# Layer 3 of a four-layer network on one Trainium2 core: mean square from moments, norm steps and output copies on ScalarE, last rows collected third quarter first

## The chip, the cores and the metric

The kernel runs on one core of one Trainium2 chip. Its engines are named as the profile names them: PE is TensorE, with PEld for its weight loads, DVE is VectorE, ACT is ScalarE, POOL is GpSimd and SP is SyncE, which here issues most of the transfers. The metric is the device time of one execution in microseconds (us), the median over several runs; lower is better.

## The reference

The input `x` has shape (4, 1024, 128) in float32. Four layers follow, each an attention-like mixer and a feed-forward part, each added to its input and followed by a layer norm without parameters. Layers 1, 2 and 3 end in a mixture of experts; the change lies in layer 3 and in the end of layer 2.

```python
def _layernorm(x, axis=-1, eps=1e-05):
    m = jnp.mean(x, axis=axis, keepdims=True)
    v = jnp.var(x, axis=axis, keepdims=True)
    return (x - m) / jnp.sqrt(v + eps)
...
# layer 2, experts: top 2 of 8, a shared matrix plus low-rank parts, 512 wide
# layer 3, mixer: query = the normed x
    rms = jnp.linalg.norm(query, axis=-1, keepdims=True) * e ** (-0.5)
    x = query / (rms + EPS)
    u = jax.nn.silu(jnp.einsum('nbe,fe->nbf', x, u_w) + u_b)
    v = jax.nn.silu(jnp.einsum('nbe,fe->nbf', x, v_w) + v_b)
...
    y = _toeplitz_mix(vh, pos, zero, neg)        # along the batch axis of 4, by head
...
    return jnp.einsum('nbf,ef->nbe', u * y, o_w) + o_b + query
# layer 3, experts: top 4 of 32, 128 wide, and a shared expert 512 wide
    logits = flat @ router_w.T + router_bias
    scores = jax.nn.softmax(logits, axis=-1)
    topk_scores, topk_idx = jax.lax.top_k(scores, TOPK)
    topk_scores = topk_scores / jnp.clip(topk_scores.sum(-1, keepdims=True), 1e-12, None)
    h = jax.nn.silu(flat @ gate_w[e]) * (flat @ up_w[e])       # for each chosen expert e
    out = sum_e topk_scores[e] * (h @ down_w[e])
    out = out + jax.nn.silu(flat @ sgate_w.T) * (flat @ sup_w.T) @ sdown_w.T
...
x = _layernorm(x + L3_attn(x)); x = _layernorm(x + L3_ffn(x))
```

The mixer of layer 3 thus works on rows that a layer norm has just left, and wants each row's root of the mean square.

## The kernel before, in words

`self.x` holds the 4096 rows in SBUF as 32 tiles of 128 rows by 128 columns; `self.xT` holds the transposed copy. The sequence is cut into four quarters of 256 positions; a quarter of all four batch rows is 8 tiles (`QT`). A tile's number is `quarter * 8 + batch_row * 2 + half`.

**Parts.** Layer 3 works in three parts: `a` is quarters 0 and 1 (16 tiles), `b` is quarter 2, `c` is quarter 3 (8 tiles each). Layer 2's experts work in parts `a2` (quarters 0 and 1), `m2` (quarters 2 and 3 of batch rows 0 and 1) and `n2` (quarters 2 and 3 of batch rows 2 and 3). Within `n2` the order is row 2: quarter 2 (indices 0, 1), quarter 3 (2, 3); row 3: quarter 2 (4, 5), quarter 3 (6, 7).

**How a mixture of experts runs.** A routing step (`l3_route`) makes logits, softmax, a top-4 mask by rounds of maximum and match-replace, and then `positions`: for each row and each of its experts, a place in a list in DRAM that is sorted by expert (`posl3a`, `posl3b`, `posl3c`; for layer 2 `posl2m` and `posl2n`), and the weights `wk`. `spread` then writes the rows of x to that list (`l3ra`, `l3rb`, `l3rc`), one indirect DMA of 128 rows at a time, 4 for a tile, issued by POOL in `indirect` (L1297). `small_experts` loads the list in groups of 4 tiles (`xg`, by SP), turns them (PE, then an ACT copy to `xgT`), multiplies by gate and up weights into `gu`, applies the activation on ACT (`sg`, L1729) and the product on DVE (`hg`, L1730), turns that (`hT`, a DVE copy, L169), multiplies by the down weights into `yp`, copies this PSUM result to `yg` and has SP store it to `l3ya`, `l3yb` or `l3yc`. Part a has 20 such groups, b and c have 12 each. The copy to `yg` is on ACT in odd groups (L1744) and on DVE in even groups (L1747). `collect` gathers a tile's results again (`yt`, again POOL, L1297, 4 indirect DMAs a tile for layer 3 and 2 for layer 2) and adds them to x, weighted, on DVE (L1388). The buffers `yt` come from a pool of 8 or 5; when they are full, the next gather waits for the adds of the oldest. Before the first group of experts there is a shared expert (`l3_shared`).

After the likely number of groups the kernel tests on the device whether the lists are longer (`rest_of`, a branch on `usedl3a` and its like). Instructions after that branch in the program can't begin before it.

**Norms.** `norm` (L185) takes a list of tiles, computes mean and variance of each with DVE's batch-norm instructions into `mv`, then `rstd`: with `by="act"` as a square root on ACT and a reciprocal on DVE (L195, L196), with `by="dve"` by three Newton steps on DVE (`rsqrt`, L171). The last step, `(x - mean) * rstd`, is one DVE instruction for each tile (L205). `finish` and `close` make the final norm and store the output.

**Layer 3's mixer** is `l3_attn` (L1548), a generator that does a quarter at a time: first norm, then for each half quarter (4 tiles) the squares and their sum on DVE (L1584, L1585), the root (Newton on DVE for part a, `exps=True`; ACT for parts b and c), the scaled rows, their transposes, the projections u and v, the mix along the batch axis on DVE (L1628), the output projection, the second norm and the transposes for the router.

**Order.** Every step is a Python generator that emits instructions and yields a planned cost in us. `mix(main, side)` advances the side generators when the main one has yielded enough cost, so the yields decide where side work lands in each engine's in-order queue. `abreast` interleaves generators by their yields, `chain` concatenates, and `press` runs side work alone until a name is listed. The part of `all` around the change, shortened:

```python
on = served(chain(rows_in(a2), onward(a, True)), (..., routed(m2)), (..., routed(n2)))
run(mix(l2_attn(1), on))
run(mix(l2_experts(m2, wall), on))
on = chain(on, rows_in(m2))
run(mix(l2_experts(n2, wall), on))
press(on, listed("l3a"))
on = chain(on, rows_in(n2), l3_attn(b), l3_route(b),
    abreast(chain(spread(b), when("made l3a"), last(a, yp)), chain(l3_attn(c), l3_route(c))),
    spread(c), when("made l3b"), last(b, yp))
run(mix(chain(l3_shared(a), l3_experts(a)), on, 0.75)); press(on, listed("l3b"))
run(mix(chain(l3_shared(b), l3_experts(b)), on, 0.75)); press(on, listed("l3c"))
run(mix(chain(l3_shared(c), l3_experts(c)), on)); run(close(c, yp))
```

`onward(a)` is part a's mixer, routing and spread. `rows_in` collects layer 2's results of a part, through a pool `l2y...` of its own with 8 buffers on the right side of SBUF; `last(a)` collects layer 3's results of part a and finishes its rows, through the pool `l3y` of 8 buffers. The yields keep POOL's order as written: spread of a, rows of m2, rows of n2, spread of b, results of a, spread of c, results of b, results of c.

Of the kernel before, what the change touches and what calls it, by code (L numbers as in the profile page):

```python
# [14 lines left out]
AF = mybir.ActivationFunctionType  # L15
ALU = mybir.AluOpType
AX = mybir.AxisListType
# [3 lines left out]
P = 128  # L21
B, L, D = 4, 1024, 128
# [8 lines left out]
QT = NT // NQT  # L31
# [10 lines left out]
E2, F2, R2, K2 = 8, 512, 16, 2  # L42
# [32 lines left out]
class Kernel:  # L75
# [106 lines left out]
            ts(t, t, -0.5, 1.5, ALU.mult, ALU.add)  # L182
            tt(y, y, t, ALU.mult)

    def norm(self, tiles, by="act"):  # L185

        nc, n = self.nc, len(tiles)
        mv = self.tile(self.small, [P, n, 2], f"mv{n}")
        for t, x in enumerate(tiles):
            st = self.tile(self.small, [P, 6], "bn")  # L190
            nc.vector.bn_stats(st, x)  # L191
            nc.vector.bn_aggr(mv[:, t, :], st)  # L192
        rstd = self.tile(self.small, [P, n], f"rstd{n}")
        if by == "act":
            nc.scalar.activation(rstd, mv[:, :, 1], AF.Sqrt, bias=self.eps)  # L195
            nc.vector.reciprocal(rstd, rstd)  # L196
        else:
            ve = self.tile(self.small, [P, n], f"ve{n}")
            nc.vector.tensor_scalar(ve, mv[:, :, 1], LN_EPS, None, ALU.add)
            if by == "pool":  # L200
                nc.gpsimd.tensor_tensor(rstd, ve, self.mhalf[:, :n], ALU.pow)
            else:
                self.rsqrt(rstd, ve)
        for t, x in enumerate(tiles):
            nc.vector.tensor_scalar(x, x, mv[:, t, 0:1], rstd[:, t : t + 1], ALU.subtract, ALU.mult)  # L205

    def quarter(self, q):

# [1165 lines left out]
                        in_=self.zero.unsqueeze(1).to_broadcast([P, tl - at, D]),  # L1374
                    )

    def collect(self, lay, part, k, yp, first=0, nt=None):

        nc = self.nc
        pos, wk = self.route[lay + part.name][:2]  # L1380
        assert f"made {lay}{part.name}" in self.listed
        ys = self.lists[lay, part.name][1]
        late = []

        def add():
            t, yt, _ = late.pop(0)
            for i in range(k):
                nc.vector.scalar_tensor_tensor(  # L1388
                    self.x[:, part.order[t], :], yt[:, i, :], wk[:, t, i : i + 1], self.x[:, part.order[t], :],
                    ALU.mult, ALU.add,  # L1390
                )

        for t in range(first, first + (nt or part.nt)):
            yt = self.tile(yp, [P, k, D], "yt")
            for i in range(k):
                self.indirect(
                    out=yt[:, i, :], out_offset=None, in_=ys,
                    in_offset=bass.IndirectOffsetOnAxis(ap=pos[:, t, i : i + 1], axis=0),
                )

            late.append((t, yt, self.moved_by + 4.0))
            if len(late) == yp.bufs:
                while late[0][2] > self.now:
                    yield (1.0,)
                add()
            yield (1.26 * k,)
        while late:
            while late[0][2] > self.now:
                yield (1.0,)
            add()  # L1410
            yield (0.36 * k,)
# [136 lines left out]
    def l3_attn(self, part, exps=False):  # L1548


        nc, tc, x, xT, col = self.nc, self.tc, self.x, self.xT, self.col
        stt = nc.vector.scalar_tensor_tensor
        NC = D13 // P
        with ExitStack() as ctx:
# [17 lines left out]
                stt(dst, pz, col["l3_b"][:, i : i + 1], dst, ALU.add, ALU.add)  # L1572

            for q in range(part.q0, part.q0 + part.nq):
                s = slice(q * QT, (q + 1) * QT)
                self.norm(self.quarter(q), by="dve" if exps else "act")
                yield (7.0,)
                xq = self.tile(vp, [P, QC], "xq")
                rms = self.tile(self.small, [P, QT], "rms")
                for g in range(2):  # L1580
                    sg = slice(q * QT + g * 4, q * QT + g * 4 + 4)
                    r = rms[:, g * 4 : g * 4 + 4]
                    sq = self.tile(vp, [P, 4, D], "sq")
                    nc.vector.tensor_tensor(sq, x[:, sg, :], x[:, sg, :], ALU.mult)  # L1584
                    nc.vector.tensor_reduce(r, sq, AX.X, ALU.add)  # L1585
                    if exps:

                        ri = self.tile(self.small, [P, 4], "rmsi")
                        v = self.tile(self.small, [P, 4], "rmsv")
                        nc.vector.tensor_scalar(v, r, 1e-30, None, ALU.max)  # L1590
                        self.rsqrt(ri, v)
                        nc.vector.tensor_tensor(r, r, ri, ALU.mult)
                    else:
                        nc.scalar.activation(r, r, AF.Sqrt)
                    nc.vector.tensor_scalar(r, r, float(np.float32(D ** -0.5)), 1e-8, ALU.mult, ALU.add)
                    nc.vector.reciprocal(r, r)
                    yield (4.0,)
                    nc.vector.tensor_tensor(sq, x[:, sg, :], r.unsqueeze(2).to_broadcast([P, 4, D]), ALU.mult)

                    stt(  # L1600
                        x[:, sg, :], x[:, sg, :], 2.0, self.row["l3_ob"].unsqueeze(1).to_broadcast([P, 4, D]),
                        ALU.mult, ALU.add,
                    )
                    yield (2.3,)
                    self.transposes(
                        ps, xq[:, g * BLK : (g + 1) * BLK], [sq[:, k, :] for k in range(4)], on_act=not exps, tag="s"
                    )
                    yield (2.3,)
                u = self.tile(vp, [P, NC, B, TQ], "u")
                for c in range(NC):  # L1610
                    v = self.tile(vp, [P, B, TQ], "v")
                    for i, dst in ((1, v), (0, u[:, c])):
                        for g in range(2):
                            pz = self.tile(ps, [P, BLK], "s")
                            self.mm(pz, wuv[:, i, c * P : (c + 1) * P], xq[:, g * BLK : (g + 1) * BLK])
                            silu(dst[:, 2 * g : 2 * g + 2, :].rearrange("p b t -> p (b t)"), pz, i * NC + c)
                            yield (2.3,)

                    cf = col["toep"][:, c * 7 : (c + 1) * 7]
                    for i in range(B):  # L1620
                        y = self.tile(vp, [P, TQ], "y", bufs=1 if exps else 2)
                        for j in range(B):
                            lag = i - j
                            a = lag if lag >= 0 else 3 - lag
                            if j == 0:
                                nc.vector.tensor_scalar(y, v[:, j, :], cf[:, a : a + 1], None, ALU.mult)
                            else:
                                stt(y, v[:, j, :], cf[:, a : a + 1], y, ALU.mult, ALU.add)  # L1628
                        if exps:
                            stt(u[:, c, i, :], u[:, c, i, :], 0.25, y, ALU.mult, ALU.mult)  # L1630
                        else:
                            nc.vector.tensor_tensor(u[:, c, i, :], u[:, c, i, :], y, ALU.mult)
                        yield (3.0,)
                for g in range(2):
                    py = self.tile(ps, [P, 4, D], "s")
                    for k in range(4):
                        b, h = (g * 4 + k) // 2, k % 2
                        for c in range(NC):
                            self.mm(py[:, k, :], u[:, c, b, h * P : (h + 1) * P], wo[:, c, :], c == 0, c == NC - 1)
                    sg = slice(q * QT + g * 4, q * QT + g * 4 + 4)  # L1640
                    nc.vector.tensor_tensor(x[:, sg, :], py, x[:, sg, :], ALU.add)
                    yield (3.0,)
                self.norm(self.quarter(q), by="dve" if exps else "act")
                yield (6.0,)
                for g in range(2):
                    self.turned(ps, q * QT + g * 4, on_act=not exps, tag="s")
                    yield (2.3,)
# [51 lines left out]
    def small_experts(self, lay, ne, part, wall):  # L1699

        nc = self.nc
# [3 lines left out]
        with ExitStack() as ctx:  # L1705
# [31 lines left out]
            def down(g):  # L1737
# [2 lines left out]
                for i in range(4):  # L1740
                    pm = self.mm(py[:, i, :], hT[:, i * P : (i + 1) * P], wall[:, bass.ds(es[i] * (3 * P) + 2 * P, P)])
                yg = self.tile(gp, [P, 4, D], "yg")
                if g % 2:
                    nc.scalar.copy(yg, py)  # L1744
                    marks = (pm,)
                else:
                    marks = (pm, nc.vector.tensor_copy(yg, py))  # L1747
# [120 lines left out]
    def all(self):  # L1868
# [4 lines left out]
        with ExitStack() as ctx:  # L1873
# [36 lines left out]
            with ExitStack() as c3:  # L1910
                with ExitStack() as c2:
# [6 lines left out]
                    self.run(self.mix(self.l2_experts(n2, wall), on, drain=False))  # L1918
                self.press(on, listed("l3a"))
                yp = self.pool(c3, "l3y", 8)  # L1920
                on = self.chain(
                    on, self.rows_in(n2), self.l3_attn(b), self.l3_route(b),
                    self.abreast(
                        self.chain(self.spread("l3", b, K3), self.when(listed("made l3a")), self.last(a, yp)),
                        self.chain(self.l3_attn(c), self.l3_route(c)),
# [192 lines left out]
```

## Time and profile before

| | us |
|---|---|
| median of 3 runs | 2064.29 (2057.93 to 2067.41) |
| the profiled execution's own time | 2440.36 |
| its span (first to last instruction), mean granted clock 0.813 | 2438.2 |
| PE busy in it | 1619.9 (66%) |
| DVE busy, 3732 instructions | 1303.3 (53%) |
| ACT busy, 1114 instructions | 789.9 (32%) |
| POOL busy, 701 instructions | 774.0 (32%) |

The profiled execution is 18% longer than the timed ones. Durations and places below are those of the profiled execution. Busy time is the time in which an engine executed instructions; shares are of the span. Stages in it: layer 2's attention, second half, ends about 1641; m2's experts run to about 1730, n2's to 1892; part a's shared expert to 1932 and its 20 groups of experts to 2034; part b's experts from 2106 to 2231; part c's to 2380; the last norms and stores end at 2438.

### The profile page before, as it was taken

The numbers are of one execution on the slowest core, as the hardware profiler recorded it, in microseconds if no ns is written. First come the engines' busy times: TensorE is split into PE (matmuls) and PEld (weight loads), VectorE is DVE, ScalarE is ACT, GpSimd is POOL, SyncE is SP. The second block draws the span as 40 slices with busy tenths as digits, with TensorE's granted clock in tenths as the row PEclk, the third lists the DMA queues.
The fourth block names the chain that finished last, engine by engine and source line by source line (L and its number), as shares of the span: only waits on it lengthen the run. The fifth ranks groups of instructions, "written<-read, shape, count | busy, mean of one in ns | idle before, by whom it ended". The sixth has DMA issues, their size and how long they took to land. (4 is left out here: it accounts for less than half of the span.)

```text
span 2438.2 us, 27135 instructions
## 1 busy us (share of the span) xinstructions
PE 1619.9 (66%) x9017; PEld 962.6 (39%) x9017; DVE 1303.3 (53%) x3732; ACT 789.9 (32%) x1114; POOL 774.0 (32%) x701
## 2 busy tenths in 40 slices
PE   7535776875661775687968787887853898267080
PEld 3214333753320344545623232345532586154070
DVE  8767795655570564324535665464711378247053
ACT  5511372322230432222336454642211254122030
POOL 5531285145227002224132002002164201736704
PEclk9766787988785888888979898988876998577595
DMA  9930002334101014312120000031141141223132
GB/s 308 288 104 0 13 33 82 117 120 159 60 31 52 14 73 142 100 48 70 44 96 21 1 1 17 2 117 35 42 174 40 44 127 45 71 71 96 51 100 59
DMA packets 215530, 187.10 MB, mean 77 GB/s; under 512 B 16528, under 2 KB 194064, under 8 KB 214864
## 3 DMA queue, kind: packets, MB, share of 16 engines
q1 hardware_dynamic: 194672, 142.29, 18.5%
q0 software_dynamic: 20704, 42.86, 5.7%
q8 instruction: 84, 1.38, 0.2%
q14 instruction: 70, 0.57, 0.1%
HBM read 88.49 MB, written 96.60 MB: 76 GB/s over the span
## 5 line engine op out<-in xcount | busy, mean ns | idle before, releaser
L1051 ACT ACTIVATE pr<-sc 128x1024 f32<-128x1024 f32 x288 | 279.6, 1021 | 326.1 <-PE sc L157 197.7
L157 PE MATMUL gu<-ld,xgT 128*128 x640 | 172.1, 413 | 81.9 <-issue 36.6
L157 PE MATMUL sc<-qm,kT 32*128 32x512 f32 (+3 forms) x1536 | 200.2, 564 | 15.9 <-ACT pr L1051 12.0
L157 PE MATMUL s<-pr,va 128*32 128x512 f32 (+3 forms) x1536 | 177.3, 531 | 46.0 <-issue 27.9
L157 PEld LDWEIGHTS gu<-ld,xgT 128*128 128x128 f32 x640 | 123.6, 204 | 109.5 <-issue 48.0
L157 PE MATMUL gu<-wall,xgT 128*128 x304 | 161.0, 657 | 3.2 <-ACT xgT L167 2.0
L1057 DVE TENSOR_TENSOR pr<-pr,ld 128x512 f32<-128x512 f32 (+1 forms) x160 | 92.5, 581 | 101.3 <-ACT pr L1051 98.8
L169 DVE COPY hT<-tp 128x512 f32<-128x512 f32 x118 | 81.0, 686 | 120.7 <-PE tp L165 50.4
L165 PE MATMUL tp<-ld,hg 128*128 128x128 f32 x624 | 100.6, 285 | 50.4 <-DVE hT L169 35.4
L157 PEld LDWEIGHTS sc<-qm,kT 32*128 32x128 f32 x1536 | 85.5, 200 | 119.5 <-issue 66.6
L165 PE MATMUL tp<-ld,xg 128*128 128x128 f32 x396 | 66.3, 295 | 90.9 <-issue 50.7
L165 PEld LDWEIGHTS tp<-ld,hg 128*128 128x128 f32 x624 | 80.1, 147 | 104.8 <-DVE hT L169 42.2
L167 ACT COPY xgT<-tp 128x512 f32<-128x512 f32 x99 | 58.0, 587 | 195.4 <-PE tp L165 126.9
L1730 DVE TENSOR_TENSOR hg<-sg,gu 128x256 f32<-128x256 f32 x160 | 65.7, 416 | 102.5 <-ACT sg L1729 94.8
L1494 ACT ACTIVATE sg<-gu 128x512 f32<-128x512 f32 x76 | 45.2, 597 | 226.3 <-PE gu L157 115.3
L1297 POOL DMA_INDIRECT l1ra<-x,posl1a x64 | 95.6, 1494 | 60.5 <-DVE posl1a L1272 41.3
L1729 ACT ACTIVATE sg<-gu 128x256 f32<-128x256 f32 x160 | 60.6, 384 | 157.3 <-PE gu L157 85.7
L157 PE MATMUL pu<-xT,ld 128*128 128x512 f32 x104 | 65.0, 719 | 60.1 <-issue 58.5
L1297 POOL DMA_INDIRECT yt<-l1yr,posl1r x64 | 60.7, 948 | 139.2 <-DVE x L1388 78.8
L157 PEld LDWEIGHTS s<-pr,va 128*32 128x32 f32 x1536 | 38.7, 113 | 156.6 <-issue 110.6
L1496 DVE TENSOR_TENSOR hg<-sg,gu 128x512 f32<-128x512 f32 x76 | 51.8, 681 | 87.2 <-ACT sg L1494 43.9
L1297 POOL DMA_INDIRECT l1rr<-x,posl1r x64 | 61.7, 964 | 99.6 <-DVE posl1r L1272 80.4
(443 smaller groups left out, 3551.7 us busy)
## 6 DMA issues: line engine op xcount, KB each, us to landing
wall<-wall SPq DMA_DIRECT2D x16, 768.0 KB
l3ra<-zero SPq DMA_DIRECT2D x1, 6144.0 KB
ld<-in_l_w SPq DMA_DIRECT2D x2, 3072.0 KB
wall<-we SPq DMA_DIRECT2D x24, 256.0 KB
ld<-in_l_w SPq DMA_DIRECT2D x1, 6144.0 KB
l1ra<-zero SPq DMA_DIRECT2D x1, 5120.0 KB
l1rr<-zero SPq DMA_DIRECT2D x1, 5120.0 KB
xg<-l3ra SPq DMA_DIRECT2D x20, 256.0 KB
```

Source lines behind the costliest of these rows:

```text
L157: return self.nc.tensor.matmul(out, lhsT, rhs, start=start, stop=stop)
L165: nc.tensor.transpose(pt[:, k * P : (k + 1) * P], s, self.ident)
L167: nc.scalar.copy(dst, pt[:, : n * P])
L169: nc.vector.tensor_copy(dst, pt[:, : n * P])
L1051: nc.scalar.activation(pr, sc[h], AF.Exp)
L1057: nc.vector.tensor_tensor(d, d, cst["tril"].unsqueeze(1).unsqueeze(1).to_broadcast([P, 2, n, P]), ALU.mult)
L1297: ins = self.nc.gpsimd.indirect_dma_start(**kw)
L1494: nc.scalar.activation(sg, gu[:, 0, :], AF.Silu)
L1496: nc.vector.tensor_tensor(h, sg, gu[:, 1, :], ALU.mult)
L1729: nc.scalar.activation(sg, pg[:, :, 0, :], AF.Silu)
L1730: nc.vector.tensor_tensor(h[:, 2 * c : 2 * c + 2, :], sg, pg[:, :, 1, :], ALU.mult)
```

## The change

Four things are changed. (1) In `l3_attn` the mean square comes from the norm's own moments: after `(x - mean) * rstd` a row's mean square is variance times rstd squared, so `rms = sqrt(var) * rstd`, 8 wide at once; the squares and their sums are gone, and in part a one Newton chain 8 wide stands in place of two 4 wide per quarter. In parts b and c both norms' last steps are ACT instructions with a scale and a bias, for which one DVE instruction makes `off = -mean * rstd`. The planned costs of these steps become smaller (7 to 6, two times 4 to one time 2, and 6 to 5). (2) The output copy `yg` of layer 3's experts is on ACT in every group. (3) `collect` can take a list of tiles, and the rows of n2 are collected with quarter 2 of both batch rows first (indices 0, 1, 4, 5); then part b's mixer and routing run abreast with the collection of quarter 3 (2, 3, 6, 7). (4) For this the pool `l3y` is used in place of n2's own pool.

```diff
--- before.py
+++ after.py
@@ -182,7 +182,8 @@
             ts(t, t, -0.5, 1.5, ALU.mult, ALU.add)
             tt(y, y, t, ALU.mult)
 
-    def norm(self, tiles, by="act"):
+    def norm(self, tiles, by="act", on_act=False):
+
 
         nc, n = self.nc, len(tiles)
         mv = self.tile(self.small, [P, n, 2], f"mv{n}")
@@ -201,8 +202,15 @@
                 nc.gpsimd.tensor_tensor(rstd, ve, self.mhalf[:, :n], ALU.pow)
             else:
                 self.rsqrt(rstd, ve)
+        if on_act:
+            off = self.tile(self.small, [P, n], f"off{n}")
+            nc.vector.scalar_tensor_tensor(off, mv[:, :, 0], -1.0, rstd, ALU.mult, ALU.mult)
         for t, x in enumerate(tiles):
-            nc.vector.tensor_scalar(x, x, mv[:, t, 0:1], rstd[:, t : t + 1], ALU.subtract, ALU.mult)
+            if on_act:
+                nc.scalar.activation(x, x, AF.Identity, bias=off[:, t : t + 1], scale=rstd[:, t : t + 1])
+            else:
+                nc.vector.tensor_scalar(x, x, mv[:, t, 0:1], rstd[:, t : t + 1], ALU.subtract, ALU.mult)
+        return mv, rstd
 
     def quarter(self, q):
 
@@ -1374,7 +1382,7 @@
                         in_=self.zero.unsqueeze(1).to_broadcast([P, tl - at, D]),
                     )
 
-    def collect(self, lay, part, k, yp, first=0, nt=None):
+    def collect(self, lay, part, k, yp, first=0, nt=None, which=None):
 
         nc = self.nc
         pos, wk = self.route[lay + part.name][:2]
@@ -1390,7 +1398,7 @@
                     ALU.mult, ALU.add,
                 )
 
-        for t in range(first, first + (nt or part.nt)):
+        for t in which or range(first, first + (nt or part.nt)):
             yt = self.tile(yp, [P, k, D], "yt")
             for i in range(k):
                 self.indirect(
@@ -1572,29 +1580,27 @@
                 stt(dst, pz, col["l3_b"][:, i : i + 1], dst, ALU.add, ALU.add)
 
             for q in range(part.q0, part.q0 + part.nq):
-                s = slice(q * QT, (q + 1) * QT)
-                self.norm(self.quarter(q), by="dve" if exps else "act")
-                yield (7.0,)
+                mv, rstd = self.norm(self.quarter(q), by="dve" if exps else "act", on_act=not exps)
+                yield (6.0,)
                 xq = self.tile(vp, [P, QC], "xq")
+
                 rms = self.tile(self.small, [P, QT], "rms")
+                if exps:
+
+                    v = self.tile(self.small, [P, QT], "rmsv")
+                    nc.vector.tensor_scalar(v, mv[:, :, 1], 1e-30, None, ALU.max)
+                    self.rsqrt(rms, v)
+                    nc.vector.tensor_tensor(rms, rms, mv[:, :, 1], ALU.mult)
+                else:
+                    nc.scalar.activation(rms, mv[:, :, 1], AF.Sqrt)
+                nc.vector.tensor_tensor(rms, rms, rstd, ALU.mult)
+                nc.vector.tensor_scalar(rms, rms, 1e-8, None, ALU.add)
+                nc.vector.reciprocal(rms, rms)
+                yield (2.0,)
                 for g in range(2):
                     sg = slice(q * QT + g * 4, q * QT + g * 4 + 4)
+                    sq = self.tile(vp, [P, 4, D], "sq")
                     r = rms[:, g * 4 : g * 4 + 4]
-                    sq = self.tile(vp, [P, 4, D], "sq")
-                    nc.vector.tensor_tensor(sq, x[:, sg, :], x[:, sg, :], ALU.mult)
-                    nc.vector.tensor_reduce(r, sq, AX.X, ALU.add)
-                    if exps:
-
-                        ri = self.tile(self.small, [P, 4], "rmsi")
-                        v = self.tile(self.small, [P, 4], "rmsv")
-                        nc.vector.tensor_scalar(v, r, 1e-30, None, ALU.max)
-                        self.rsqrt(ri, v)
-                        nc.vector.tensor_tensor(r, r, ri, ALU.mult)
-                    else:
-                        nc.scalar.activation(r, r, AF.Sqrt)
-                    nc.vector.tensor_scalar(r, r, float(np.float32(D ** -0.5)), 1e-8, ALU.mult, ALU.add)
-                    nc.vector.reciprocal(r, r)
-                    yield (4.0,)
                     nc.vector.tensor_tensor(sq, x[:, sg, :], r.unsqueeze(2).to_broadcast([P, 4, D]), ALU.mult)
 
                     stt(
@@ -1640,8 +1646,8 @@
                     sg = slice(q * QT + g * 4, q * QT + g * 4 + 4)
                     nc.vector.tensor_tensor(x[:, sg, :], py, x[:, sg, :], ALU.add)
                     yield (3.0,)
-                self.norm(self.quarter(q), by="dve" if exps else "act")
-                yield (6.0,)
+                self.norm(self.quarter(q), by="dve" if exps else "act", on_act=not exps)
+                yield (5.0,)
                 for g in range(2):
                     self.turned(ps, q * QT + g * 4, on_act=not exps, tag="s")
                     yield (2.3,)
@@ -1740,7 +1746,7 @@
                 for i in range(4):
                     pm = self.mm(py[:, i, :], hT[:, i * P : (i + 1) * P], wall[:, bass.ds(es[i] * (3 * P) + 2 * P, P)])
                 yg = self.tile(gp, [P, 4, D], "yg")
-                if g % 2:
+                if lay == "l3" or g % 2:
                     nc.scalar.copy(yg, py)
                     marks = (pm,)
                 else:
@@ -1918,8 +1924,13 @@
                     self.run(self.mix(self.l2_experts(n2, wall), on, drain=False))
                 self.press(on, listed("l3a"))
                 yp = self.pool(c3, "l3y", 8)
+
                 on = self.chain(
-                    on, self.rows_in(n2), self.l3_attn(b), self.l3_route(b),
+                    on, self.collect("l2", n2, K2, yp, which=(0, 1, 4, 5)),
+                    self.abreast(
+                        self.chain(self.l3_attn(b), self.l3_route(b)),
+                        self.collect("l2", n2, K2, yp, which=(2, 3, 6, 7)),
+                    ),
                     self.abreast(
                         self.chain(self.spread("l3", b, K3), self.when(listed("made l3a")), self.last(a, yp)),
                         self.chain(self.l3_attn(c), self.l3_route(c)),
```

## The prediction

> **What bounds the kernel now.** I read the page's busy shares first, then the windows of 50 us over the part that the change touches, then the waits there, then the queue of POOL.
>
> ```profile
> PE 1619.9 (66%) x9017; PEld 962.6 (39%) x9017; DVE 1303.3 (53%) x3732; ACT 789.9 (32%) x1114; POOL 774.0 (32%) x701
> ```
>
> No engine is full over the span, so the stages have to be read one by one. Nothing moves before the second half of layer 2's attention, so only the last 900 us matter. Columns of the next view: stretch, its length, busy time of PE, PEld, DVE, ACT and POOL with instruction counts, granted clock, DMA share, GB/s.
>
> ```profile
> 1900.00:1950.00 50.00, 42.95 (x204) 29.59 (x204) 16.90 (x36) 9.64 (x18) 15.25 (x16) 0.90 0.17 48
> 1950.00:2000.00 50.00, 45.86 (x292) 39.76 (x291) 34.40 (x94) 30.24 (x55) 0.00 (x0) 1.00 0.43 129
> 2000.00:2050.00 50.00, 44.23 (x252) 36.09 (x251) 40.19 (x128) 25.07 (x42) 0.00 (x0) 0.87 0.22 65
> 2050.00:2100.00 50.00, 29.51 (x116) 16.80 (x114) 24.91 (x91) 11.08 (x17) 27.67 (x28) 0.79 0.12 44
> 2100.00:2150.00 50.00, 8.97 (x20) 4.94 (x20) 13.01 (x36) 3.41 (x6) 35.87 (x37) 0.55 0.27 75
> 2250.00:2300.00 50.00, 8.94 (x43) 5.85 (x41) 1.20 (x3) 0.60 (x1) 37.81 (x41) 0.60 0.20 59
> ```
>
> Two kinds of stage alternate. From 1932 to 2037 layer 3's experts of part a run: PE is busy for 45.9 of 50 us, DVE for 34 to 40, ACT for 25 to 30. What DVE gives up there buys nothing by itself. Around 2100 and 2275 PE has 9 of 50 us and POOL 36 to 38: POOL issues gathers and scatters one after another, and everything else waits for their data. The waits and the instructions of the scatter of part b's rows (`l3rb`) say what holds POOL up:
>
> ```profile
> POOL l3rb L1297 <- DVE posl3b L1272: 119.1, 1, 119.1
> POOL yt L1297 <- DVE x L1388: 78.9, 7, 53.3
> POOL l3ra L1297 <- DVE posl3a L1272: 67.4, 1, 67.4
> ...
> L1297 POOL DMA_INDIRECT l3rb<-x,posl3b x32: 957/962/1262, 2064.1 to 2104.2; - x32
> L1328 SPq DMA_DIRECT2D xg<-l3rb x12: 359/360/1177, 2106.5 to 2198.8; - x12
> ```
>
> POOL stood idle for 119.1 us until DVE had computed `posl3b`, part b's positions in its experts' lists. Then came 32 scatters of 1.26 us spacing (0.96 busy, 0.30 of issue), ending at 2105, and at 2106.5 the first load of part b's expert rows. So the way from part a's last expert to part b's first is: `posl3b`, 32 scatters, load. PE fills little of it. Its own timeline:
>
> ```profile
> 2033.84 0.28 PE L157 MATMUL yp<-ld,hT 128*128 x1
> 2039.36 2.18 PE L165 MATMUL s<-ld,x 128*128 128x128 f32 x8 [5.25 <-DVE x L205]
> ...
> 2067.18 3.17 PE L157 MATMUL py<-ld,hs 128*128 128x128 f32 x26 [0.32 <-DVE hs L736]
> ...
> 2109.62 0.69 PE L165 MATMUL tp<-ld,xg 128*128 128x128 f32 x2 [10.26 <-issue]
> ```
>
> Part a's experts end at 2034. Part b's second norm (L205) is only then done, so its transposes (L165 `s`) start at 2039; logits, softmax, top-4 and positions follow, and the shared expert of b is over by 2070. From there to 2109 PE has 13 matmul groups of part c's attention and nothing else.
>
> **What the Trainium skill says.** "Perfetto Trace Analysis", section "Identifying Performance Opportunities", says that the busiest engine may change from regime to regime, and that one then looks for its gaps and for whoever ends them: that is the reading above, and the trace agrees (46 of 50 us of PE, then 9). The same page, section "DMA Instruction — SWDGE (GPSIMD)", says that such an instruction's end is the end of descriptor generation and not of the move; here the load follows 1.3 us after the last scatter's end, so little is hidden in that. "ScalarE: Activation LUTs", section "What ACT_TABLE_LOAD costs", gives 1283 ns for a table load, as in this trace (1.28 us), and a price for the moved norm step, which the trace before does not show in that form (below).
>
> **The change, part by part.** Order of instructions is taken from both programs, engine by engine; POOL's order is the same in both, and SP's nearly so.
>
> *Part b's routing moves ahead.* Now part b's second norm, logits, softmax, top-4 and weights stand behind the branch that ends part a's experts; in the changed program they stand ahead of it, and about 12 small position operations remain behind it. This comes from the smaller planned costs of layer 3's attention (24.2 to 17.2 for a quarter's first steps, 6 to 5 for its second norm) and from starting part b's attention after four of n2's eight tiles of rows. Before, from the branch at 2038.8 to the first scatter at 2064.1 it took 25.3 us. Twelve operations of 0.2 to 0.35 us with two crossings between PE and DVE take some 8 us (my estimate from these rows). So the scatters start 17 us earlier. PE's gap from 2070 to 2109 is longer than that, so nothing else takes its place: -17 in the profiled execution.
>
> *Part a's routing moves ahead too*, by 12 to 19 us at `posl3a` by the same count. But part a's scatters ended at 1843 and its experts began only at 1932, behind n2's experts and the shared expert. What is late next is PE itself, so I give this -3; bounds 0 and -15 (n2's experts stand still at 1767 to 1781 and 1805 to 1872 while POOL scatters, and a shorter overlap would let them go on).
>
> *DVE loses work.* Part a, two quarters: 2 squarings, 2 reductions of 0.69 us and some 17 small Newton steps of 0.2 each, 6 us a quarter, 12 in all. Parts b and c: 2.8 us for the squares, 2 x 2.1 us for two norms' last steps (8 x 0.27, L205), 14 for both. Output copies: 22 x 0.69 = 15. Together 41 of 1303 us. In experts(a) PE covers it (45.9 of 50), in attention(1) PE and ACT do. In part c's experts (2343 to 2380) DVE is the busier one, and 6 copies leave it: -2; bounds 0 and -8 for the whole.
>
> *ACT gains work.* 22 copies of 0.58 us, 13 us, and 32 norm steps of 128x128 with two pointers. By the page these take 186 + 107 + 2 x 93 = 479 ns, 386 back to back: 12 us, an estimate; the nearest row, rstd on 128x8, has 0.30, which would make 10. Eight table loads fewer give back 10 us. Net 15 us on an engine with 790 of 2438, 25 to 30 of 50 in the crowded stage: room is there, but each norm puts 3.1 us in a row ahead of the experts' `sg`, and `off` adds one DVE step. Cost +1; bounds 0 and +12 (four bursts that each stop PE for 3 us).
>
> *Queued behind the moved work.* DVE gets part a's top-4 in one piece (match-replace on 16 tiles 2.75 us each round, MAX8 1.59) between m2's expert groups, so `hT` and `hg`, on which PE waits, come later; PE gets 8 transposes, logits and masks of part b, about 5 us, inside experts(a). It is work moved from elsewhere, yet PE was full here and idle there: +4; bounds 0 and +15.
>
> *The gathers of layer 2's last rows* take their buffers from the layer-3 pool. Before, the first of them waited 53.3 us for the adds that free memory. They now can go earlier, hidden beside part a's shared expert: 0; bounds -5 and 0.
>
> **Sum.** -17 -3 -2 +1 +4 = -17 in the profiled execution, so 2440.4 us to about 2423. That execution is 18% longer than the timed runs (median 2064.3), and much of the excess seems to be stalls in just these POOL stretches; scaled by 0.846 the 17 becomes 14.4, and with the idle time of norm chains less distorted I take 16: **2048 us**.
>
> **The rivals.**
>
> *The gain is given back (same).* POOL takes things in order: behind `l3rb` stand 64 gathers of part a's results, where it waited 26.0 us for DVE's adds (L205, L1388), and only then part c's 32 scatters. If those adds don't come earlier, part b's experts start 17 us sooner, but part c's rows don't. For it: c's end hangs on `l3rc` (2228 to 2273). Against: the adds that free the buffers need only the gathers, which move along. Gain 0 to 8 us: 2056 to 2064. Chance 0.19.
>
> *Bursts stop PE (slower).* PE, ACT and DVE are in-order queues, and norm, transposes and logits of part b enter experts(a) with ACT in the chain. If each of some eight hand-overs (two norms, two turns, logits, softmax, mask, and part a's top-4 in m2) stops PE for 4 us, 32 us are lost against the 17 gained: 15 slower, 2079. It decides from 2 us each. For it: PE is at 45.9 of 50 there. Against: two groups are kept in flight, and the windows leave DVE 10 us in 50 and ACT 20. Chance 0.16.
>
> *Both scatters' moves count (faster still).* If `posl3a` gates as well (its scatters no longer stand beside n2's stalled experts) and the DVE savings shorten the chains: -17 -15 -8 = -40, scaled -34: about 2030, down to 2015. Chance 0.23.
>
> *The forecast*, 2038 to 2054: chance 0.42.
>
> **Numbers.** About 0.5% (10 us) is what a measurement of this kernel can tell from no change. Faster by more: 0.42 + 0.23 = 0.65; within: 0.19; slower: 0.16. The range takes in both ends, from 2016 (the larger gain with both bounds used) to 2078 (the bursts); where faster holds, 2020 to 2054.
>
> **What would show it.** Right: the first `l3rb` scatter within 12 us of part a's last expert matmul, POOL's wait for `posl3b` shorter than 119 by at least 15, the gap of PE ahead of part b's first `tp` shorter, 57 table loads where there were 65, DVE near 1262 busy. Wrong: experts(a) longer than 105 us by 10 or more (bursts), `l3rc` starting no earlier against part a's end (given back), or experts(a) starting over 10 us earlier against the end of attention (both count).

## The result and the profile after

The changed kernel takes 2031.69 us (median of 5 runs, 2027.95 to 2041.13) against 2064.29 before (5 runs). The measured ratio is 0.9871, 95% interval 0.9845 to 0.9897, so 1.3% or 27 us faster (21 to 32 by the interval); the two medians lie 33 us apart. Gains below are such ratios, in us of the kernel before. On some chips both kernels take about 2430 us instead of 2060, with PE, DVE and ACT standing still together beside POOL's indirect transfers (last section); the profile of before is from such a chip and that of after is not, so each ratio below is against the kernel before on the same chip, and stages are compared only between traces of one kind.

The busy times of the page after, in the columns of the line shown of before:

```profile
PE 1547.3 (76%) x9017; PEld 936.7 (46%) x9017; DVE 1272.9 (62%) x3630; ACT 803.5 (39%) x1159; POOL 782.3 (38%) x701
```

DVE has 102 instructions fewer and 30 us less busy time; ACT has 45 more and 14 us more. The windows after (stretch, length, PE, PEld, DVE, ACT, POOL, clock, DMA share, GB/s); part a's experts now lie between 1641 and 1741:

```profile
1650.00:1700.00 50.00, 47.81 (x288) 40.05 (x287) 33.78 (x96) 32.23 (x66) 3.83 (x5) 1.00 0.39 118
1700.00:1750.00 50.00, 42.17 (x268) 35.76 (x266) 36.20 (x142) 30.77 (x61) 0.00 (x0) 0.92 0.25 75
1750.00:1800.00 50.00, 33.86 (x137) 19.08 (x135) 26.21 (x68) 10.74 (x17) 34.83 (x34) 0.88 0.14 52
1900.00:1950.00 50.00, 33.00 (x157) 24.51 (x156) 11.86 (x24) 11.24 (x23) 37.81 (x41) 0.80 0.35 107
```

PE still sets the pace among part a's experts (47.8 of 50 us). The two waits of POOL that the forecast named, from the waits of after:

```profile
POOL l3rb L1305 <- ACT sg L743: 100.1, 1, 100.1
...
POOL l3ra L1305 <- DVE posl3a L1280: 35.7, 1, 35.7
```

The page of before had 67.4 and 119.1 us here, but on a chip of the other kind. No trace of the kernel before was taken on a chip near 2060; the nearest is the kernel before with 12 of part a's scatters left out (described below, the "cut kernel"):

```profile
POOL l3rb L1297 <- DVE posl3b L1272: 108.3, 1, 108.3
POOL l3ra L1297 <- DVE posl3a L1272: 52.1, 1, 52.1
```

Against it the waits are 16.4 and 8.2 us shorter. The length of such a wait also depends on when POOL becomes free, so the starts of stages below say more. The wait for part b is put down to an ACT instruction, presumably because ACT now writes part b's x, which the scatter reads; `posl3b` had ended 0.7 us before.

### The profile page after: what moved, and what is told of

Read it like the earlier page. It is cut to its first block, busy times and chain, and to the rows that moved or that the text cites. A ratio compares the mean times of both kernels' runs of the same rounds, so it can differ in the third digit from the quotient of the medians.

```text
span 2039.3 us, 27065 instructions
## 1 busy us (share of the span) xinstructions
PE 1547.3 (76%) x9017; PEld 936.7 (46%) x9017; DVE 1272.9 (62%) x3630; ACT 803.5 (39%) x1159; POOL 782.3 (38%) x701
## 5 line engine op out<-in xcount | busy, mean ns | idle before, releaser
L157 PE MATMUL sc<-qm,kT 32*128 32x512 f32 (+3 forms) x1536 | 189.0, 546 | 1.0 <-ACT pr L1059 1.0
L157 PE MATMUL gu<-ld,xgT 128*128 x640 | 164.6, 400 | 22.4 <-DVE hg L1736 13.6
L157 PE MATMUL s<-pr,va 128*32 128x512 f32 (+3 forms) x1536 | 161.7, 516 | 19.9 <-DVE x L997 7.3
L157 PE MATMUL gu<-wall,xgT 128*128 x304 | 147.9, 611 | 2.7 <-ACT xgT L167 2.0
L1305 POOL DMA_INDIRECT l1rr<-x,posl1r x64 | 66.0, 1031 | 101.4 <-DVE posl1r L1280 82.2
L165 PE MATMUL tp<-ld,xg 128*128 128x128 f32 x396 | 66.3, 294 | 37.0 <-DMA xg<-l3rc 12.5
L157 PE MATMUL yp<-ld,hT 128*128 x640 | 87.1, 278 | 4.0 <-DVE hT L169 2.2
L1305 POOL DMA_INDIRECT l2rm<-x,posl2m x16 | 15.9, 994 | 193.3 <-DVE posl2m L1280 188.8
L1305 POOL DMA_INDIRECT yt<-l1ya,posl1a x64 | 69.3, 1083 | 51.2 <-DMA l1ya<-yg 22.0
```

The costliest lines, as they stand in the source:

```text
L157: return self.nc.tensor.matmul(out, lhsT, rhs, start=start, stop=stop)
L165: nc.tensor.transpose(pt[:, k * P : (k + 1) * P], s, self.ident)
L1305: ins = self.nc.gpsimd.indirect_dma_start(**kw)
```

## The experiments

**The kernel before, profiled again**, twice and unchanged.

> The kernel before, unchanged, profiled once more, for a profile whose own time is near the timed median of 2064. All theories read from it where POOL and PE wait in the last 500 us: the order theory expects 20 to 28 us from the branch behind part a's experts to the first l3rb scatter, and PE with little to do until those scatters end; a gap below 12 us would leave that theory nothing to gain.

> The kernel before, unchanged, for one more profile. In the first such profile PE, DVE and ACT stood still together in places while POOL issued indirect transfers, some 400 us in all, and its own time was 2432. Either these stalls come back (a time near 2430) or they don't (a time near 2064); in the second case the 25 us from the branch behind part a's experts to the first l3rb scatter should still be there, if the order theory holds.

Both came out near 2430 (2431.57 and 2429.92), with the stalls. From PE's load of the count of part a's lists (the branch behind its experts) to the first `l3rb` scatter there were 30.5 us in the first (2023.4 to 2053.9), so the gap that the forecast counted on is there.

**Three parts of the change alone**, all on one chip near 2430. The order of rows:

```diff
-                    on, self.rows_in(n2), self.l3_attn(b), self.l3_route(b),
+                    on, self.collect("l2", n2, K2, yp, which=(0, 1, 4, 5)),
+                    self.abreast(
+                        self.chain(self.l3_attn(b), self.l3_route(b)),
+                        self.collect("l2", n2, K2, yp, which=(2, 3, 6, 7)),
+                    ),
```

> Only the order of n2's rows: third quarter first, part b's mixer and routing abreast with the rest, gathers through the pool l3y. In the program 34 DVE instructions instead of 51 stand between the branch behind part a's experts and posl3b (18 with the whole change). Order theory (the gain is part b's routing moved ahead of that branch): 8 to 14 us faster. Work theory (the gain is DVE work that is gone or moved to ACT): 0 to 4 us. Buffer theory (n2's gathers no longer wait for memory of m2's): 10 us or more, and the same for the pool alone.

The mixer (the hunks of `norm` and `l3_attn`, nothing else):

> Only the mixer: mean square from the moments, both norms' last step on ACT in parts b and c, and the smaller planned costs. Output copies and order of rows as before. 44 instead of 51 DVE instructions stand behind the branch ahead of posl3b, 12 instead of 36 ahead of posl3a. Order theory: 4 to 10 us faster, by what stands behind the branches. Work theory: 14 to 22 us faster. Buffer theory: about 0.

The copies:

```diff
-                if g % 2:
+                if lay == "l3" or g % 2:
```

> Only the output copies of layer 3's experts, all on ACT. Order theory: 0 to 3 us faster, PE sets the pace of these stages. Work theory: 5 to 10 us faster (22 copies of 0.69 us leave DVE). Buffer theory: 0.

Measured: rows 1.0060 (1.0041 to 1.0079), 15 us slower; mixer 0.9946 (0.9928 to 0.9964), 13 us faster; copies 0.9975 (0.9960 to 0.9990), 6 us faster. Here the order theory misses the rows by more than 20 us, and the mixer and the copies by 3 each. The work theory gets the copies, misses the mixer by 1 us and the rows wholly. Yet the new order of rows does shorten the way from PE's load behind the branch to part b's first scatter, from 30.5 us to 19.4 in its trace; its loss must lie elsewhere. Of the buffer theory the sign is wrong and the size striking, so the next run took the pool alone.

**The pool alone**, on a chip near 2440:

```diff
-                    on, self.rows_in(n2), self.l3_attn(b), self.l3_route(b),
+                    on, self.collect("l2", n2, K2, yp), self.l3_attn(b), self.l3_route(b),
```

> Only the buffers: n2's rows are gathered in the old order, through the pool l3y in place of their own, so that their first gather no longer waits for memory that m2's gathers use. All else as before. Buffer theory: this alone brings most of what the whole change brings where the order of the rows does, and most of what it costs where it costs (rows alone was 0.6% slower at times near 2430): the same 0.6%. Order theory: 0 to 2 us either way, since 51 DVE instructions still stand behind the branch ahead of posl3b. Work theory: 0.

1.0063 (1.0041 to 1.0085), 15 us slower: the pool alone costs as much as the new order of rows with its pool. Two traces show where. First `n2`'s gathers on POOL in the first profile repeated of before, then in the pool's run (op, count, shortest, median and longest ns, first and last start):

```profile
L1297 POOL DMA_INDIRECT yt<-l2yn,posl2n x16: 940/944/1069, 1906.7 to 1934.0; - x16
```

```profile
L1297 POOL DMA_INDIRECT yt<-l2yn,posl2n x16: 940/944/947, 1908.2 to 1926.9; - x16
```

Before, these 16 gathers are broken up by waits for DVE's adds, whose buffers they take over. With the other pool they run back to back, and 12 us after their start PE stops in the middle of part a's shared expert (timeline of PE, the pool's run; the bracket is the idle time ahead and who ended it):

```profile
1932.27 2.08 PE L157 MATMUL pu<-xT,ld 128*128 128x512 f32 x2 [11.81 <-DVE hs L736]
```

Before, PE runs through this expert without a stop. DVE, on which PE waits, stands still in both, with a releaser that the profile calls "remote", that is none that it can name: before for 6.3 us at the expert's end, behind the last 8 gathers without a pause, and in the pool's run for 17.5 us.

```profile
1928.49 0.69 DVE L1687 TENSOR_TENSOR x<-py,x 128x512 f32<-128x512 f32 x1 [6.28 <-remote]
```

```profile
1930.93 0.69 DVE L1687 TENSOR_TENSOR x<-py,x 128x512 f32<-128x512 f32 x1 [17.54 <-remote]
```

The length of the stage repeats this in every trace near 2430. From the last store of n2's results to the first load of part a's expert rows it takes 45.7 to 45.9 us in all seven without the new pool, and 56.4 (pool), 56.6 (rows) and 55.4 (whole change) with it, some 10 us more; where the rest of the 15 us goes was not followed. A wait that was taken away here had kept POOL's stream broken.

**The whole change again, without the rows, and the planned costs alone**, on one chip near 2430.

> The whole change, timed again. Order theory: where the engines don't stand still beside POOL, 20 to 35 us faster than before, as measured first; where they do (times near 2430), part b's earlier routing is worth less, since what runs beside POOL's scatters stands still: 5 to 20 us faster. Work theory: 20 to 35 us in both cases, DVE's and ACT's saved work doesn't depend on POOL.

> The whole change without the new order of n2's rows and without the pool l3y for them: mixer and copies only. 42 DVE instructions stand behind the branch ahead of posl3b, against 18 with the whole change and 51 before. Order theory: of a gain of 27 us at most 15 are left. Work theory: 22 us or more are left.

The costs alone:

```diff
-                yield (7.0,)
+                yield (6.0,)
...
-                    yield (4.0,)
+                    if g == 0:
+                        yield (2.0,)
...
-                yield (6.0,)
+                yield (5.0,)
```

> Only the smaller planned costs (7 to 6, twice 4 to once 2, 6 to 5), no instruction removed or moved to another engine. 47 instead of 51 DVE instructions stand behind the branch ahead of posl3b, 12 instead of 36 ahead of posl3a. Order theory: 2 to 8 us faster, most of what the mixer's change alone brings. Work theory: 0.

The whole change 0.9981 (0.9968 to 0.9995), 5 us faster; without rows 0.9964 (0.9947 to 0.9981), 9 us faster (mixer and copies alone had given 13 and 6 on another chip of this kind, so they don't add up); costs 0.9984 (0.9968 to 1.0000), 4 us. The work theory, which wanted 20 us or more on every chip, is out: the same program gains 27 us on one kind of chip and 5 on the other. The costs' interval reaches to no change. Their trace still tells something: `posl3a` comes 16 us earlier, counted from part m2's first scatter, by the smaller planned costs alone as by the whole mixer, so in this kind that move is one of order and not of work.

Why the change brings 22 us less in this kind is shown only in part. The whole change has the 13.6 us from PE's load behind the branch to part b's first scatter here too. Some 10 us go in the stage with the new pool, as above. Another 10 or so go between part c's first scatter and its first load of rows: 107.7 to 112.0 us in the three traces with the mixer's part, 98.5 to 102.9 in the seven without it. Nothing like the latter shows near 2060 (41.7 and 44.3 us, with the mixer's part and in the cut kernel), and its cause stays open.

**The change without the mixer's part**, this time on a chip near 2060.

> The whole change without the mixer's part: the new order of n2's rows with the pool l3y, and the copies on ACT; squares, norms and planned costs as before. 33 DVE instructions stand behind the branch ahead of posl3b (51 before, 18 with the whole change), 36 ahead of posl3a, as before. If times lie near 2430: the pool costs 15 us as in its own run, the copies give 6, the earlier posl3b little: 6 to 12 us slower than before (buffer theory). If times lie near 2064: order theory 10 to 20 us faster, work theory 3 to 8 us faster.

0.9954 (0.9934 to 0.9975): rows and copies bring 9.5 us, between what the work theory (3 to 8) and the order theory (10 to 20) wanted, and its interval, 5 to 14 us, takes in parts of both. So some 17 of the 27 hang on the mixer's part; how much of that its planned costs alone would bring near 2060 was not run. Its trace against that of after shows where. Both reach the end of n2's experts at the same time (last store of n2's results at 1594.5 and 1592.7), yet part a's first expert rows load at 1655.8 and 1641.5. First without the mixer's part, then the whole change:

```profile
L1517 SPq DMA_DIRECT2D l2yn<-yg x5: 359/360/377, 1550.4 to 1594.5; - x5
L1328 SPq DMA_DIRECT2D xg<-l3ra x20: 359/360/497, 1655.8 to 1728.5; - x20
```

```profile
L1525 SPq DMA_DIRECT2D l2yn<-yg x5: 359/360/377, 1547.8 to 1592.7; - x5
L1336 SPq DMA_DIRECT2D xg<-l3ra x20: 359/360/504, 1641.5 to 1712.6; - x20
```

The timeline of DVE in part a's shared expert, without the mixer's part, and what PE waited for:

```profile
1630.82 0.35 DVE L1388 SCALAR_TENSOR_TENSOR x<-yt,wkl2m,x 128x128 f32<-128x128 f32 x1 [13.31 <-DMA yt<-l2ym,posl2m]
1633.34 0.61 DVE L1388 SCALAR_TENSOR_TENSOR x<-yt,wkl2m,x 128x128 f32<-128x128 f32 x2 [2.16 <-DMA yt<-l2ym,posl2m]
1634.72 0.35 DVE L1388 SCALAR_TENSOR_TENSOR x<-yt,wkl2m,x 128x128 f32<-128x128 f32 x1 [0.77 <-DMA yt<-l2ym,posl2m]
1634.99 1.28 DVE L736 TENSOR_TENSOR hs<-sg,pu 128x512 f32<-128x512 f32 x2
```

```profile
1635.72 2.08 PE L157 MATMUL pu<-xT,ld 128*128 128x512 f32 x2 [15.51 <-DVE hs L736]
```

And the whole change, the same two places:

```profile
1617.67 0.35 DVE L1396 SCALAR_TENSOR_TENSOR x<-yt,wkl2m,x 128x128 f32<-128x128 f32 x1 [1.94 <-DMA yt<-l2ym,posl2m]
```

```profile
1622.43 2.02 PE L157 MATMUL pu<-xT,ld 128*128 128x512 f32 x2 [3.99 <-DVE hs L744]
```

The adds of m2's rows stand in DVE's queue in the middle of the shared expert, ahead of the products `hs` that PE needs. The first add waits for a gather, and POOL issues that gather only behind the 64 scatters of part a, which wait for `posl3a`. So a late `posl3a` stops DVE for 13.3 us, and PE behind it for 15.5. With `posl3a` at 1526 instead of 1540 this shrinks to 1.9 and 4.0, and the stage from n2's last store to part a's first rows from 61.3 us to 48.8.

**That wait by itself**, two kernels on one chip near 2060: the kernel before and the changed kernel, each with the last 12 scatters of part a left out and all planned times kept.

```diff
+            gone = lay + part.name == "l3a" and t >= 13
+            if gone:
+                self.moved_by = max(self.moved_by, self.now) + 1.26 * k
-            for i in range(k):
+            for i in range(0 if gone else k):
```

> The kernel before, with 12 of the 64 scatters of part a's rows left out (the last three tiles never reach part a's list, so their experts get zeros); every other instruction and its order as before. POOL thus reaches m2's gathers 15 us earlier, as it does by an earlier posl3a in the whole change. New theory, from the traces of the whole change and of no_attn: in part a's shared expert DVE stands at the first add of m2's results until POOL has done the scatters of part a and the first gather (13.3 us, with PE behind it 15.5), and the mixer's part gains by cutting this. It expects 9 to 13 us faster where times lie near 2064, and the 13 us wait gone from the trace. The forecast's step (PE alone is late there) expects 0 to 3 us. Where times lie near 2430, n2's experts end later and the wait is not there: 0 to 8 us for both, from fewer stalls.

> The whole change with the same 12 scatters left out. New theory: only about 2 us of DVE's wait and 4 of PE's are left to remove, so 0 to 4 us on top of the whole change's 27 where times lie near 2064; if scatters cost time in another way than by this wait, the same 9 to 13 us on top.

The kernel before gains 18 us: 0.9912 (0.9885 to 0.9940), more than the 9 to 13 expected but with the PE wait measured above (15.5) inside its interval. The add finds its data: in its timeline the first add has no wait, the next 1.1 us, and the stage from n2's last store to part a's first rows takes 44.1 us.

```profile
1616.33 0.34 DVE L1391 SCALAR_TENSOR_TENSOR x<-yt,wkl2m,x 128x128 f32<-128x128 f32 x1
1617.78 0.62 DVE L1391 SCALAR_TENSOR_TENSOR x<-yt,wkl2m,x 128x128 f32<-128x128 f32 x2 [1.11 <-DMA yt<-l2ym,posl2m]
```

The changed kernel with the same cut is at 0.9837 (0.9812 to 0.9862), 34 us below before. The two gains alone, 18 and 27, would add up to 45; 11 us are missing, because both take away the same wait: the stage from n2's last store to part a's first rows is 61.3 us without the mixer's part, 12.5 less with it and 17.2 less with the scatters left out, but only 18.5 less with both, 11 short of the sum. On top of the whole change it is 7 us, measured in different runs with overlapping intervals, against an expected 0 to 4; the stage goes from 48.8 to 42.8. This is no better version, since rows are left out; whether DVE's adds can be placed later without delaying part b was not tried.

**The stages**, as starts of instructions in us from the first scatter of part m2, traces of chips near 2060. The cut kernel before has before's order from part a's experts on and stands in for it there.

| first start of | before, cut | rows and copies only | whole change |
|---|---|---|---|
| part a's scatters | 214.5 | 217.7 | 206.2 |
| part a's expert rows | 312.5 | 332.9 | 321.2 |
| part b's scatters | 435.8 | 450.9 | 434.8 |
| part b's expert rows | 478.0 | 493.0 | 479.0 |
| part c's scatters | 562.5 | 577.0 | 563.8 |
| end (last store of the output issued) | 709.6 | 722.0 | 708.9 |

From part a's expert rows to part b's scatters it takes 123.3, 118.0 and 113.6 us; from there to the end 273.8, 271.1 and 274.1. So after the shared expert the whole change gains 9.7 us in one place, ahead of `posl3b`, and nothing later. How much of the 118.0 is the rows and how much the copies was not run apart on such a chip. The 11.7 us by which part a's expert rows load earlier than without the mixer's part and these 9.7 make 21 of the 27 us; the rest has no place in these traces, and is no more than the measurement's interval.

## Why the prediction was right, and where it was not

**Direction and size.** 16 us were forecast; the ratio gives 27 and the medians 33. The range held it, but the measured 2031.69 lies outside the forecast's own band, 2038 to 2054, and beside the rival in which both scatters' moves count, about 2030. That rival's sign came as well: by the table part a's expert rows load 11.7 us earlier than without the mixer's part. Its reason did not, since n2's experts end at the same time in both. There is luck in the size too: the sum of 17 us was worked out for the kind of chip in the read profile, where the change brings 5, and scaling carried it over to the other kind, where a large part of the gain comes from a wait that the read profile did not have.

**Part b's routing ahead of the branch: right.** The forecast cut 17 us from the branch to the first scatter. It counted from 2038.8, where DVE starts behind the branch; from PE's load its profile has 30.7 us where it says 25.3. PE's load behind the branch and the scatters and loads of part b, first in the cut kernel before, then in the whole change:

```profile
L1357 PEldq TENSOR_LOAD <-usedl3a x1: 312/312/312, 1731.0 to 1731.0; - x1
```

```profile
L1297 POOL DMA_INDIRECT l3rb<-x,posl3b x32: 954/958/1191, 1760.8 to 1800.4; - x32
```

```profile
L1362 PEldq TENSOR_LOAD <-usedl3a x1: 315/315/315, 1741.5 to 1741.5; - x1
```

```profile
L1305 POOL DMA_INDIRECT l3rb<-x,posl3b x32: 957/962/1947, 1755.1 to 1796.8; - x32
L1336 SPq DMA_DIRECT2D xg<-l3rb x12: 359/360/500, 1799.2 to 1841.6; - x12
```

29.8 us became 13.6, 16.2 less; on a chip near 2430 the whole change has 13.6 as well. The scatters start 12.9 us after part a's last expert matmul ends, just over the 12 that the prediction named as a sign. The work moved ahead lengthened part a's experts from 93.5 us (1637.5 to 1731.0) to 100.0: 6.5, where +1 and +4 were booked. Net 9.7 us, where 12 were expected. The bursts of the slower rival can be at most these 6.5, a fifth of its price.

**Part a's routing ahead: the step that failed.** The prediction saw `posl3a` 12 to 19 us earlier (it is 14) and went on: "What is late next is PE itself, so I give this -3". What was late next was DVE, at an add that waits for POOL's gather behind part a's scatters; this term is 12 us by PE's wait (15.5 to 4.0) and by the stages (332.9 to 321.2). It lies within the bound of -15, but that bound was set for n2's stalled experts, not for this wait. The profile that was read did not have the wait. On that chip n2's experts themselves stood still beside the scatters and ended at 1892, long after the scatters, and from their last store to part a's first rows it took 45.9 us, about as in the cut kernel (44.1); on the chips of the timed runs they end before the scatters do, and the stage takes 61.3. The prediction did note that the profiled execution was 18% longer by stalls in these stretches, but scaled its sum for it instead of asking which waits the stalls hid.

**DVE's work: the size.** 41 us were expected to go, 30.2 went (1303.1 in the cut kernel before, 1272.9). The sum took 0.69 us for each operation; but two `hs` in a row, 0.69 us each, take 1.28 in the DVE lines above, so instructions in a row overlap, here by 0.1 us, and busy time counts the overlap once. Summed one by one, DVE's durations fell by 39.8 us (1499.4 to 1459.5), nearly the 41; so the work that went was counted rightly, and 10 us of it had never been busy time of its own. That it buys little fits the stages: part b's 12 groups take 50.2 us between first and last load in the cut kernel and 50.6 with all copies on ACT, and while the whole change has 42.4 there, its way from part b's scatters to the end is no shorter (274.1 and 273.8 us).

**ACT's work: right.** The Trainium skill's price ("ScalarE: Activation LUTs", "What ACT_TABLE_LOAD costs") gave an estimate of 479 ns for a norm step; the group of after shows 488 for the 32 of them, and eight in a row took 3.19 us against the 3.1 predicted.

```profile
L210 ACT ACTIVATE x<-x,off,rstd 128x128 f32<-128x128 f32 x32 | 12.9, 488 | 0.6 <-DVE off L207 0.6
```

Table loads fell from 64 to 57; the 57 was predicted, from a count of 65 that was one too high. ACT's busy time rose by 14 us, where 15 were expected.

**n2's buffers: the sign was open and I closed it.** The prediction gave the shared pool 0, with bounds of -5 and 0. On the chips near 2430, the kind that was read, it costs 15 us, outside these bounds; on the others it was not run alone.

## What to carry to other kernels

When a step moves on one in-order queue, follow the queue on: here POOL's scatters delayed a gather, the gather an add on DVE, and the add stood ahead of a product that PE needed; it took two traces of stages side by side to see it. A wait in a queue that is not the bound can protect others, so price its removal from both sides. When the profiled execution is much longer than the timed ones, its waits are those of another schedule: look for the waits that its stalls cover before scaling a sum.

## What the runs showed of the hardware

The same program took 2031.69 us and, on another chip, 2428.60. By the two traces PE, DVE and ACT are idle at the same time for 132 us in the first and 438 in the second (between the first and the last instruction of the three), and some 240 of the 306 us more lie inside stretches where POOL issues four or more indirect transfers in a row, at the same pace in both (0.96 us busy each). In the whole change's profile on the slower chip POOL scatters part a's rows from 1739 to 1829 and goes on with gathers to 1850, and from 1805 on PE stops for 39 us:

```profile
L1305 POOL DMA_INDIRECT l3ra<-x,posl3a x64: 956/962/1330, 1739.2 to 1828.7; - x64
```

```profile
1844.76 1.12 PE L165 MATMUL tp<-ld,hg 128*128 128x128 f32 x4 [39.32 <-DVE hT L169]
```

```profile
1844.02 0.69 DVE L169 COPY hT<-tp 128x512 f32<-128x512 f32 x1 [49.07 <-remote]
```

DVE, on which PE waited, had itself been idle for 49.1 us, again with "remote" in place of a releaser, and on the faster chip the three engines are never idle together for more than 0.3 us beside part a's scatters. What the engines lack there the profile does not show, nor what sets the two kinds of chip apart. That it is bound to POOL's unbroken streams is not proven: it rests on their places in these traces and on the pool's run, in which 16 gathers without a pause came with a stop of PE of 11.8 us inside the shared expert, and DVE's stop grew from 6.3 to 17.5 us.
